# Layer 1's linear attention: mean of the values outside the product, and its products in half-array tiles side by side

## Chip, cores and metric

The kernel runs on one core of a Trainium2 chip. The metric is device time in microseconds, the median over executions. TensorE (PE) multiplies matrices and writes PSUM; VectorE (DVE), ScalarE (ACT) and GpSimd (POOL) do elementwise work; SyncE (SP) only issues transfers here. All data is float32.

## The reference, cut to what matters

Four layers follow each other on `x` of 2 x 512 x 32 x 32: deformable attention with an MLP (layer 0), linear attention (layer 1), and two multi-head attentions behind a group norm (layers 2 and 3). The change is in layer 1:

```python
Q = einsum('oc,bcn->bon', wq, xf) + bq          # 64 x 1024 per batch
K = einsum('oc,bcn->bon', wk, xf) + bk
V = einsum('oc,bcn->bon', wv, xf) + bv          # 512 x 1024
Q = Q / norm(Q, axis=1);  K = K / norm(K, axis=1)
k_sum  = K.sum(-1) + 1e-6
tailor = 1.0 / (n + einsum('bnm,bm->bn', Qt, k_sum))
v_sum  = V.sum(-1)
matrix = einsum('bmn,bcn->bmc', K, V)
matrix_sum = v_sum[:, :, None] + einsum('bnm,bmc->bcn', Qt, matrix)
return x + gamma * (matrix_sum * tailor[:, None, :])
```

The values V are never formed: `matrix` is K times x, and that times the weights of V.

## The kernel before

`xs[b][t]` holds x: two batches, four tiles `t` of 128 channels by 1024 points. A point block `n` is 128 points (eight a batch). The weights of layer 1 lie in `w` as 128 rows x 4 tiles x 640 columns: 512 for V, 64 for Q, 64 for K. The functions are nested in `layer1`, and an order written out by hand at its end fixes what TensorE, ACT and DVE do one after the other (`manual_schedule`); POOL's order and SP's transfers are left to the scheduler.

- `queries_keys(b, half)` (L1062): queries and keys with points on partitions, 16 products for four point blocks; DVE adds the bias, ACT squares.
- `unit_length(b)` (L1084): sums of squares on DVE, square root on ACT, reciprocal on DVE; normed keys `kn` and queries `qn`. Both have a 65th column of ones, so that one product carries the sum of the values along.
- `turned_x(b)` (L1096): x transposed by TensorE, 32 tiles of 128 x 128 a batch; ACT and DVE copy them out, alternately.
- `keys_sum(b)` (L1109) spreads the sum of the keys over all partitions by a product with ones; `keys_column(b)` (L1117) gets the same sum as a column.
- `keys_x(b)` (L1126): x times keys, 32 products with 128 columns of x as weights and the 65 columns of `kn` streamed; result in four tiles `m1`.
- `divisors(b)` (L1143): the divisor of each query, on DVE, and the queries divided by it.
- `turned(b, h)` (L1162) transposes the queries; `matrix(b)` (L1170) multiplies `m1` by the weights of V, 65 rows of 512.
- `result(b, h, t)` (L1181): one product with 65 rows per half and tile. For batch 0 DVE adds it to x, for batch 1 ACT copies it out and POOL adds.

PSUM has three banks in pool `ps`, three in `ps_q`, and two single ones in `ps_m` (tags `m1` and `s`). Interleaved with batch 1 stand the steps of layer 2's group norm on batch 0: `channel_means` (statistics of a tile on DVE), `group_means` (two small products) and `norm_first`, which makes the first operand of layer 2's first product `qk20P`. On POOL the weight sums of layer 2 (L869 to L872) stand before and between the fills of layer 1's constants.

Of the kernel before, what the change touches and what calls it, by code (L numbers as in the profile page):

```python
# [36 lines left out]
    ("gamma1", 1),  # L37
# [19 lines left out]
class Net:  # L57
# [980 lines left out]
    def layer1(self, w, bias):  # L1038
# [3 lines left out]
        with ExitStack() as ctx:  # L1042
# [10 lines left out]
            xT, qk, qn, kn = [], [], [], []  # L1053
            for b in range(B):
                qn.append(pool.tile([P, NB, P], F32, tag=f"qn{b}", name=f"qn{b}"))
                kn.append(pool.tile([P, NB, DH + 1], F32, tag=f"kn{b}", name=f"kn{b}"))
                nc.gpsimd.memset(qn[b][:, :, DH:P], 1.0)
                nc.gpsimd.memset(kn[b][:, :, DH : DH + 1], 1.0)

            sqs = []  # L1060

            def queries_keys(b, half):  # L1062

                if half == 0:
                    qk.append(pool.tile([P, NB, 2, DH], F32, tag=f"qk{b}", name=f"qk{b}"))
                qk_ps = ps_q.tile([P, 4, P], F32, tag="ps", name=f"l1qk{b}{half}")
                for i in range(4):
                    n = 4 * half + i
                    for t in range(CT):
                        xt = self.xs[b][t][:, n * P : (n + 1) * P]  # L1070
                        nc.tensor.matmul(
                            qk_ps[:, i, :], lhsT=xt, rhs=w[:, t, C:640], start=(t == 0), stop=(t == CT - 1)
                        )
                nc.vector.tensor_tensor(
                    qk[b][:, 4 * half : 4 * half + 4, :, :].rearrange("p n a d -> p n (a d)"),
                    qk_ps,
                    bias[:, C:640].unsqueeze(1).to_broadcast([P, 4, P]),
                    ALU.add,
                )
                if half:  # L1080
                    sqs.append(pool.tile([P, NB, 2, DH], F32, tag=f"sq{b}", name=f"sq{b}"))
                    nc.scalar.activation(sqs[b], qk[b], AF.Square)

            def unit_length(b):  # L1084
                r = small.tile([P, NB, 2], F32, tag="r", name=f"r{b}")
                nc.vector.tensor_reduce(r, sqs[b], AX.X, ALU.add)
                nc.scalar.activation(r, r, AF.Sqrt)
                nc.vector.reciprocal(r, r)
                nc.vector.tensor_tensor(
                    kn[b][:, :, 0:DH], qk[b][:, :, 1, :], r[:, :, 1:2].to_broadcast([P, NB, DH]), ALU.mult  # L1090
                )
                nc.vector.tensor_tensor(
                    qn[b][:, :, 0:DH], qk[b][:, :, 0, :], r[:, :, 0:1].to_broadcast([P, NB, DH]), ALU.mult
                )

            def turned_x(b):  # L1096
                xT.append(pool.tile([P, NB, C], F32, tag=f"xT{b}", name=f"xT{b}"))
                for n in range(NB):
# [5 lines left out]
                    (nc.scalar.copy, nc.vector.tensor_copy)[n % 2](xT[b][:, n, :], tr)  # L1104

            vec, act = nc.vector, nc.scalar
            m1, mats, q_at, kbs, kss = [], [], [], [], []

            def keys_sum(b):  # L1109

                kb_ps = ps_m.tile([P, DH + 1], F32, tag="s", name=f"kb{b}")
                for n in range(NB):
                    nc.tensor.matmul(kb_ps, lhsT=ones, rhs=kn[b][:, n, :], start=(n == 0), stop=(n == NB - 1))
                kbs.append(small.tile([P, DH + 1], F32, tag="kb", name=f"kbs{b}"))
                vec.tensor_scalar(kbs[b], kb_ps, 1e-6, None, ALU.add)

            def keys_column(b):  # L1117
                s_ps = ps_m.tile([P, DH + 1], F32, tag="s", name=f"s{b}")
                for n in range(NB):
                    nc.tensor.matmul(  # L1120
                        s_ps[0 : DH + 1, 0:1], lhsT=kn[b][:, n, :], rhs=ones[:, 0:1], start=(n == 0), stop=(n == NB - 1)
                    )
                kss.append(small.tile([DH + 1, 1], F32, tag="ks", name=f"ks{b}"))
                vec.tensor_copy(kss[b], s_ps[0 : DH + 1, 0:1])

            def keys_x(b):  # L1126

                m1_ps = ps_m.tile([P, CT, DH + 1], F32, tag="m1", name=f"m1{b}")
                m1.append(pool.tile([P, CT, DH + 1], F32, tag=f"m1{b}", name=f"m1s{b}"))
                for t in range(CT):  # L1130
                    for n in range(NB):
                        nc.tensor.matmul(
                            m1_ps[:, t, :],
                            lhsT=xT[b][:, n, t * P : (t + 1) * P],
                            rhs=kn[b][:, n, :],
# [3 lines left out]
                    if t == CT - 1:  # L1139
                        act.copy(m1[b], m1_ps)  # L1140
                    yield

            def divisors(b):  # L1143

                prod = pool.tile([P, NB, DH], F32, tag=f"prod{b}", name=f"prod{b}")
                vec.tensor_tensor(
                    prod, qn[b][:, :, 0:DH], kbs[b][:, 0:DH].unsqueeze(1).to_broadcast([P, NB, DH]), ALU.mult
                )
                d = small.tile([P, NB], F32, tag="d", name=f"d{b}")
                vec.tensor_reduce(d, prod, AX.X, ALU.add)  # L1150
                yield
                vec.tensor_scalar(d, d, float(N), None, ALU.add)
                vec.reciprocal(d, d)
                vec.tensor_scalar(d, d, self.col("gamma1"), None, ALU.mult)
                vec.tensor_tensor(
                    qn[b][:, :, 0 : DH + 1],
                    qn[b][:, :, 0 : DH + 1],
                    d.unsqueeze(2).to_broadcast([P, NB, DH + 1]),
                    ALU.mult,
                )  # L1160

            def turned(b, h):  # L1162
                tr = ps_q.tile([P, HF], F32, tag="ps", name=f"qt{b}{h}")
                for n in range(4):
                    nc.tensor.transpose(tr[:, n * P : (n + 1) * P], qn[b][:, 4 * h + n, :], self.ident)
                qa = pool.tile([DH + 1, HF], F32, tag=f"qa{b}{h}", name=f"qa{b}{h}")
                act.copy(qa, tr[0 : DH + 1, :])
                q_at.append(qa)

            def matrix(b):  # L1170
                m_ps = ps_m.tile([DH + 1, C], F32, tag="m1", name=f"m{b}")
                for t in range(CT):
                    nc.tensor.matmul(m_ps, lhsT=m1[b][:, t, :], rhs=w[:, t, 0:C], start=(t == 0), stop=(t == CT - 1))
                mat = pool.tile([DH + 1, C], F32, tag=f"mat{b}", name=f"mat{b}")
                for cut in (slice(0, C // 2), slice(C // 2, C)):
                    vec.scalar_tensor_tensor(
                        mat[:, cut], bias[0 : DH + 1, cut], kss[b], m_ps[:, cut], ALU.mult, ALU.add
# [3 lines left out]
            def result(b, h, t):  # L1181
                w_ps = ps.tile([P, HF], F32, tag="ps", name=f"w{b}{h}{t}")
                nc.tensor.matmul(
                    w_ps, lhsT=mats[b][:, t * P : (t + 1) * P], rhs=q_at[2 * b + h], start=True, stop=True
                )
                xt = self.xs[b][t][:, h * HF : (h + 1) * HF]
                if b == 0:
                    vec.tensor_tensor(xt, w_ps, xt, ALU.add)
                else:

                    ws = last.tile([P, HF], F32, tag="ws", name=f"ws{h}{t}")
                    act.copy(ws, w_ps)
                    nc.gpsimd.tensor_tensor(xt, xt, ws, ALU.add)
# [4 lines left out]
            with self.tc.manual_schedule(engines=engines):  # L1198
                for b, half in ((0, 0), (0, 1), (1, 0)):
                    queries_keys(b, half)  # L1200
                unit_length(0)
                queries_keys(1, 1)
                for b in range(B):
                    turned_x(b)
                unit_length(1)
                keys_sum(0)
                for _ in divisors(0):
                    pass
                for _ in keys_x(0):
                    pass  # L1210
                keys_column(0)
                turned(0, 0)
                matrix(0)
                turned(0, 1)
                keys_sum(1)

                divided, summed = divisors(1), keys_x(1)
                for t in range(CT):
                    for h in range(2):
                        result(0, h, t)  # L1220
                    self.channel_means(2, 0, t)
                    next(summed)
                    if t in (0, 2):
                        next(divided, None)
                next(summed, None)
                keys_column(1)
                turned(1, 0)
                matrix(1)
                turned(1, 1)
                steps = self.group_means(2, 0, ps_m.tile([P, 2, 5 * CT], F32, tag="s", name="gm2"))  # L1230
                next(steps)
                for h in range(2):
                    for t in range(CT):
                        result(1, h, t)
                        if h == 0 and t == 2:
                            next(steps, None)
                        elif h == 1 and t == 1:
                            self.norm_first(2)
# [720 lines left out]
def _layout(i):  # L1959
# [10 lines left out]
    def over(v):  # L1970
# [14 lines left out]
        "gamma1": over(l1["gamma"]),  # L1985
# [45 lines left out]
```

## Time and profile before

| what | value |
|---|---|
| median of 3 runs | 3259.72 us (3259.31 to 3261.21) |
| the profiled execution: time, span | 3260.07 us, 3258.3 us |
| granted TensorE clock in it | 1.0 |
| layer 1 on TensorE | 2342.58 to 2406.57 us |
| busy in 2342.50 to 2406.60: PE, DVE, ACT, POOL | 63.99, 34.48, 16.05, 15.91 us |

The profile is of one execution. Time around the span (start and end of the program) makes the 1.8 us between span and time. A line such as `L1183` is a line of the kernel; `w<-qa,mat` reads as output and inputs; `65*128` is the part of the array that the weights take, `65x512` what is streamed. A float32 product shows as two records, a transpose as one. Matmul records overlap: a record's own duration is longer than the distance to the next, and the distance is what TensorE's time is made of. In the chain of waits a piece has its start, its length and its line.

### The profile page before, as it was taken

To read this page: it belongs to the slowest core of one execution; us is meant where nothing else is said; L and a number is where in the kernel's file an instruction comes from. 1 tells how busy PE (TensorE), PEld (TensorE's weight loads), DVE (VectorE), ACT (ScalarE), POOL (GpSimd) and SP (SyncE) were. 2 spreads that over 40 slices of the span, in tenths; PEclk is the share of its full clock that TensorE was granted. 3 is DMA by queue.
4 is the path that set the end of the run, shared out by engine and by line. 5 is a ranking of instruction groups with operands and counts; after the bars stand their busy time and mean duration, and the time that the engine had idled before them with its cause. 6 is when DMAs were issued, how large, how long until landed. Compare 5 with 4: busy or idle time off the path is not lost.

```text
span 3258.3 us, 59109 instructions
## 1 busy us (share of the span) xinstructions
PE 3243.6 (100%) x24496; PEld 1210.7 (37%) x24496; DVE 2388.4 (73%) x2742; ACT 1949.1 (60%) x2013; POOL 2348.2 (72%) x1557
## 2 busy tenths in 40 slices
PE   9999999999999999999999999999999999999999
PEld 4333333333333333332333334444555533455333
DVE  7877878878877778878877765475555689855897
ACT  7787887887886687887887752111121466213662
POOL 7998998999998698999999972442323458634575
PEclk9999999999999999999999999999999999999999
DMA  6676776667766476667676662111000100000001
GB/s 171 144 152 136 152 148 143 146 146 146 149 145 127 104 153 139 142 143 146 149 145 145 145 158 78 39 39 39 1 1 1 40 1 2 14 1 14 1 1 53
DMA packets 96571, 309.35 MB, mean 95 GB/s; under 512 B 14688, under 2 KB 16864, under 8 KB 93216
## 3 DMA queue, kind: packets, MB, share of 16 engines
q0 software_dynamic: 57040, 200.31, 32.5%
q1 hardware_dynamic: 38240, 103.05, 9.7%
q8 instruction: 197, 3.23, 0.4%
q10 hardware_dynamic: 1008, 2.06, 0.2%
q14 instruction: 86, 0.70, 0.1%
HBM read 67.33 MB, written 4.46 MB: 22 GB/s over the span
## 4 chain that ended last, share of the span: by engine, by line
PE 81%; POOL 11%; DVE 5%; issue 2%; ACT 0%; DMA 0%; DVEq 0%; POOLq 0%; ACTq 0%; SPq 0%
PE hp L704 41%; PE s L1569 5%; PE o L1598 5%; POOL h L723 5%; POOL h L720 4%; PE qk30P L1344 1%; PE qk20P L1344 1%; PE m_7P L899 1%; PE m_6P L899 1%; PE m_4P L899 1%; PE m_2P L899 1%; PE m_0P L899 1%; PE qk31P L1344 1%; PE qk21P L1344 1%; PE m_5P L899 1%
## 5 line engine op out<-in xcount | busy, mean ns | idle before, releaser
L704 PE MATMUL hp<-h,w2s 128*32 128x512 f32 x16384 | 1784.0, 592 | 0.5 <-DVE h L680 0.2
L680 DVE CUSTOM_DVE_ANT_1 h<-tx,bank 128x1024 f32<-128x1024 f32 (+1 forms) x1028 | 1180.3, 1210 | 301.9 <-PE hp L704 240.3
L709 ACT ACTIVATE h<-hp,magb 128x1024 f32<-128x1024 f32 x1024 | 1133.1, 1110 | 378.8 <-PE hp L704 368.2
L704 PEld LDWEIGHTS hp<-h,w2s 128*32 128x32 f32 x16384 | 530.6, 110 | 1212.5 <-issue 1184.6
L720 POOL TENSOR_TENSOR h<-h,h 128x1024 f32<-128x1024 f32 x255 | 819.1, 3212 | 1.6 <-ACT h L709 1.6
L723 POOL TENSOR_TENSOR h<-h,h 128x1024 f32<-128x1024 f32 x254 | 751.3, 2958 | 0.0
L716 POOL DMA_DIRECT2D h<-h x255 | 303.0, 1188 | 192.3 <-ACT h L709 179.6
L1573 ACT ACTIVATE e<-s 128x1024 f32<-128x1024 f32 x256 | 262.0, 1025 | 181.1 <-PE s L1569 176.5
L711 ACT ACTIVATE h<-h,flip 128x1024 f32<-128x1024 f32 x256 | 294.3, 1150 | 8.4
L1598 PE MATMUL o<-e,v 64*64 64x512 f32 x2048 | 265.2, 589 | 2.2 <-DVE q L1637 2.2
L1569 PE MATMUL s<-q,k 64*64 64x512 f32 x2048 | 265.9, 591 | 0.0
L1580 POOL TENSOR_TENSOR some<-some,e 128x1024 f32<-128x1024 f32 x64 | 168.2, 2629 | 26.2 <-ACT e L1573 23.3
L1578 POOL TENSOR_TENSOR some<-e,e 128x1024 f32<-128x1024 f32 x32 | 76.1, 2379 | 141.3 <-DVE sum L1587 102.3
L726 POOL DMA_DIRECT2D h<-h x127 | 175.4, 1381 | 1.0 <-issue 1.0
L725 POOL DMA_DIRECT2D h<-h x127 | 149.0, 1173 | 0.0
L1585 DVE TENSOR_TENSOR sum<-sum,e 128x1024 f32<-128x1024 f32 x64 | 124.6, 1947 | 28.8 <-ACT e L1573 26.1
L869 POOL TENSOR_TENSOR mlp_w<-mlp_w 128x512 f32<-128x512 f32 x16 | 22.3, 1391 | 165.0 <-DMA mlp_w<-in_mlp_w 111.2
L1598 PEld LDWEIGHTS o<-e,v 64*64 64x64 f32 x2048 | 77.8, 133 | 145.1 <-issue 134.9
L1569 PEld LDWEIGHTS s<-q,k 64*64 64x64 f32 x2048 | 76.5, 133 | 133.2 <-issue 117.5
L960 ACT ACTIVATE mh<-mh,cols 128x512 f32<-128x512 f32 x64 | 46.1, 721 | 124.3 <-DVE mh L978 65.4
L1583 DVE TENSOR_TENSOR sum<-e,e 128x1024 f32<-128x1024 f32 x32 | 81.5, 2547 | 31.7 <-ACT e L1573 31.6
L1332 POOL TENSOR_TENSOR sq<-q 128x512 f32<-128x512 f32 x32 | 33.2, 1041 | 96.1 <-DVE q L1351 54.2
(572 smaller groups left out, 3365.2 us busy)
## 6 DMA issues: line engine op xcount, KB each, us to landing
h<-h POOLq DMA_DIRECT2D x255, 512.0 KB, 5.4
h<-h POOLq DMA_DIRECT2D x254, 256.0 KB, 5.0
h<-h SPq DMA_DIRECT2D x127, 256.0 KB, 4.0
lb<-logs SPq DMA_DIRECT2D x63, 512.0 KB, 5.6
mlp_w<-in_mlp_w SPq DMA_DIRECT2D x16, 1024.0 KB, 4.9
x<-in_x SPq DMA_DIRECT2D x8, 512.0 KB, 7.5
qkw<-in_l_qk SPq DMA_DIRECT2D x2, 2048.0 KB, 7.7
out<-x SPq DMA_DIRECT2D x15, 256.0 KB, 2.0
```

Of the source, the lines that this page charges most:

```text
L680: self.nc.vector._custom_dve(TENSOR_ADD_SAT, out=h1[r][:, k, cut, :], in0=x[:, 4 * half + 2 * r + k, :].unsqueeze(1).to_broadcast([P, H // ...
L704: nc.tensor.matmul(hp[rows, cut], lhsT=self.l0w2[:, 32 * q : 32 * q + 32], rhs=h1[k][:, cut], start=True, stop=True)
L709: nc.scalar.activation(y, hp, AF.Relu, bias=self.magb[:, q, 0:1])
L711: nc.scalar.activation(y, y, AF.Copy, scale=self.flip)
L716: nc.gpsimd.dma_start(y, ys[0], accum_op=ALU.add)
L720: (nc.vector if final else nc.gpsimd).tensor_tensor(y, y, ys[2], ALU.add)
L723: (nc.vector if final else nc.gpsimd).tensor_tensor(z, z, other, ALU.add)
L726: nc.gpsimd.dma_start(z[1::2, :], z[0::2, :], accum_op=ALU.add)
L899: self.nc.tensor.matmul(acc[p], lhsT=w[:, a, k, p * P : (p + 1) * P], rhs=right(r, k), start=k == 0, stop=k == 1)
L1569: nc.tensor.matmul(s[halves[c], par, :], lhsT=ks[p][rows, at : at + DH], rhs=qs[p][rows, cut], start=True, stop=True)
L1573: nc.scalar.activation(e, s, AF.Exp, scale=DH**-0.5)
L1598: nc.tensor.matmul(o[halves[par], r, :], lhsT=v[n // 2][rows, n % 2, at : at + DH], rhs=e[rows, par, :], start=(n == 0), stop=(n == NB - 1),)
```

## The change

The sum of the values no longer rides along as row 65. With c the mean of x over the points, V's sum is n times (wv c + bv), and the result is gamma (wv c + bv) plus gamma times the divided queries times a matrix that is built from x - c. ACT takes minus the means (`means_less`), `means_row` and `means_columns` turn them into the constant column `rest` that is added with the result, and `centred` subtracts the means' share from keys times x. Keys and queries then have 64 columns, and `keys_x`, `matrix` and `result` are each two products on halves of the array. In `keys_x` and `matrix` the halves are two groups of 64 columns; in `result` they are two groups of 64 rows, for which the divided queries are written twice. Divisors move to POOL (`divided`), batch 0's tiles 2 and 3 are added on ACT and POOL, batch 1's tiles 0 and 1 on DVE. The order by hand is new.

```diff
-            qn.append(pool.tile([P, NB, P], ...)); kn.append(pool.tile([P, NB, DH + 1], ...))
-            nc.gpsimd.memset(qn[b][:, :, DH:P], 1.0)
-            nc.gpsimd.memset(kn[b][:, :, DH : DH + 1], 1.0)
+            less = pool.tile([P, CT, 32], F32, tag="less", name="l1less")
+            gps.memset(less, 0.0)
...
+            def means_less(b):
+                for t in range(CT):
+                    act.activation(spare, self.xs[b][t], AF.Copy, scale=-1.0 / N, accum_out=less[:, t, b : b + 1])
...
-            def keys_column(b):
...
+            def divided(b):
+                prod = sqs[b][:, :, 0, :]
+                gps.tensor_tensor(prod, qk[b][:, :, 0, :], kbs[b].unsqueeze(1).to_broadcast([P, NB, DH]), ALU.mult)
+                d = small.tile([P, NB], F32, tag="d", name=f"d{b}")
+                vec.tensor_reduce(d, prod, AX.X, ALU.add)
+                vec.tensor_scalar(d, d, float(N), None, ALU.add)
+                vec.reciprocal(d, d)
+                vec.tensor_scalar(d, d, self.col("gamma1"), None, ALU.mult)
+                qn.append(pool.tile([P, NB, 2, DH], F32, tag=f"qn{b}", name=f"qn{b}"))
+                for i in range(2):
+                    gps.tensor_tensor(
+                        qn[b][:, :, i, :], qk[b][:, :, 0, :], d.unsqueeze(2).to_broadcast([P, NB, DH]), ALU.mult
+                    )
...
             def keys_x(b):
-                for t in range(CT):
-                    for n in range(NB):
+                for n in range(NB):
+                    for half in range(2):
                         nc.tensor.matmul(
-                            m1_ps[:, t, :],
-                            lhsT=xT[b][:, n, t * P : (t + 1) * P],
-                            rhs=kn[b][:, n, :],
+                            m1_ps[half * DH : (half + 1) * DH, :],
+                            lhsT=kn[b][:, n, :],
+                            rhs=xT[b][:, n, half * 2 * P : (half + 1) * 2 * P],
...
+            def centred(b):
+                tr = ps_m.tile([P, 2, P], F32, tag="m1", name=f"m1t{b}")
+                for j in range(2):
+                    nc.tensor.transpose(tr[:, j, :], m1[b][:, j * P : (j + 1) * P], self.ident)
+                m1[b] = pool.tile([P, CT, DH], F32, tag=f"m1c{b}", name=f"m1c{b}")
+                for t in range(CT):
+                    vec.scalar_tensor_tensor(
+                        m1[b][:, t, :], kbs[b], less[:, t, b : b + 1],
+                        tr[:, t % 2, (t // 2) * DH : (t // 2 + 1) * DH], ALU.mult, ALU.add,
+                    )
...
             def matrix(b):
-                    nc.tensor.matmul(m_ps, lhsT=m1[b][:, t, :], rhs=w[:, t, 0:C], start=(t == 0), stop=(t == CT - 1))
+                    for half in range(2):
+                        nc.tensor.matmul(
+                            m_ps[half * DH : (half + 1) * DH, :],
+                            lhsT=m1[b][:, t, :],
+                            rhs=w[:, t, half * 2 * P : (half + 1) * 2 * P],
...
+            def means_row():
+                got = ps_m.tile([P, C], F32, tag="s", name="l1row")
+                for t in range(CT):
+                    nc.tensor.matmul(
+                        got[32 * t : 32 * t + 32, :], lhsT=less[:, t, :], rhs=w[:, t, 0:C], start=True, stop=True
+                    )
...
+            def means_columns(row):
+                got = ps_m.tile([P, CT, B], F32, tag="s", name="l1cols")
+                for t in range(CT):
+                    nc.tensor.matmul(got[:, t, :], lhsT=row[:, t * P : (t + 1) * P], rhs=pick, start=True, stop=True)
+                for b in range(B):
+                    vec.tensor_tensor(rest[:, b, :], self.colr("vb1", CT), got[:, :, b], ALU.subtract)
+                vec.tensor_scalar(rest, rest, self.col("gamma1"), None, ALU.mult)
+
+            def result(b, j, h):
+                for half, to in enumerate((ps, ps_q)):
+                    t = 2 * half + j
+                    rows = slice(half * DH, (half + 1) * DH)
+                    w_ps = to.tile([P, HF], F32, tag="ps", name=f"w{b}{h}{t}")
+                    nc.tensor.matmul(
+                        w_ps, lhsT=mats[b][rows, j * P : (j + 1) * P], rhs=q_at[2 * b + h][rows, :], start=True, stop=True
+                    )
+                    xt = self.xs[b][t][:, h * HF : (h + 1) * HF]
+                    more = rest[:, b, t : t + 1]
+                    if half == 0:
+                        vec.scalar_tensor_tensor(xt, w_ps, more, xt, ALU.add, ALU.add)
+                    else:
+                        ws = last.tile([P, HF], F32, tag="ws", name=f"ws{b}{h}{t}")
+                        act.activation(ws, w_ps, AF.Identity, bias=more)
+                        gps.tensor_tensor(xt, xt, ws, ALU.add)
...
+                queries_keys(0, 0)
+                means_less(0)
+                queries_keys(0, 1)
+                queries_keys(1, 0)
                 unit_length(0)
+                means_less(1)
                 queries_keys(1, 1)
+                keys_sum(0)
+                turned_x(0, range(NB))
                 unit_length(1)
+                divided(0)
+                keys_x(0)
+                row = means_row()
+                turned_x(1, range(0, 4))
+                centred(0)
+                keys_sum(1)
+                turned_x(1, range(4, NB))
+                matrix(0)
                 turned(0, 0)
                 turned(0, 1)
+                means_columns(row)
+                divided(1)
+                for j in range(2):
+                    for h in range(2):
+                        result(0, j, h)
+                keys_x(1)
+                for t in (0, 2):
+                    self.channel_means(2, 0, t)
                 turned(1, 0)
+                turned(1, 1)
+                centred(1)
+                for t in (1, 3):
+                    self.channel_means(2, 0, t)
                 matrix(1)
                 steps = self.group_means(2, 0, ps_m.tile([P, 2, 5 * CT], F32, tag="s", name="gm2"))
+                result(1, 0, 0)
                 next(steps)
+                result(1, 0, 1)
+                next(steps, None)
+                result(1, 1, 0)
+                self.norm_first(2)
+                result(1, 1, 1)
```

The packed table `cols` of per-channel constants gains the four columns of V's bias (`vb1`), 156 in place of 152.

## The prediction

> **What bounds the kernel now.** I read the page first. TensorE is busy for the whole span, and the chain that ended last runs 81% on it.
>
> ```profile
> PE 3243.6 (100%) x24496; PEld 1210.7 (37%) x24496; DVE 2388.4 (73%) x2742; ACT 1949.1 (60%) x2013; POOL 2348.2 (72%) x1557
> PE 81%; POOL 11%; DVE 5%; issue 2%; ACT 0%; DMA 0%; DVEq 0%; POOLq 0%; ACTq 0%; SPq 0%
> ```
>
> The change lies in layer 1, so next the chain cut to the stretch between the last MLP product and the first two products of layer 2.
>
> ```profile
> 2342.58 14.29 PE l1qk L1071 x128
> 2356.87 6.99 PE l1t L1101 x64
> 2363.86 1.73 PE kb L1113 x16
> 2365.59 7.15 PE m L1132 x64
> 2372.74 0.89 PE s L1120 x16
> ...
> 2374.13 3.43 PE m L1173 x8
> ...
> 2399.24 2.81 PE w L1183 x6
> 2402.05 0.12 PE gm L1493 x2
> 2402.18 4.40 PE w L1183 x10
> 2406.57 6.44 PE qk20P L1344 x15
> ```
>
> Layer 1 is 2342.58 to 2406.57, 64.0 us, with one piece (0.11 us) that is not a product: TensorE alone sets its length. A float32 product is two records here, a transpose one. Pitches: 128 columns of weights cost 0.11 us however little streams past (7.15 / 64), 512 streamed columns 0.43 us (3.43 / 8). So the stage gets shorter by what TensorE loses, until a product has to wait. What could make it wait is read from the other engines' timelines:
>
> ```profile
> 2347.16 2.36 POOL L871 TENSOR_TENSOR qkm<-qkw 128x1024 f32<-128x1024 f32 x1
> 2349.46 0.20 POOL L1052 MEMSET l1ones<- 128x128 f32 x1
> 2350.49 1.06 ACT L1082 ACTIVATE sq<-qk 128x1024 f32<-128x1024 f32 x1 [27.83 <-DVE qk L1074]
> 2351.56 1.28 ACT L1087 ACT_TABLE_LOAD   x1
> ```
>
> POOL reaches layer 1's fills only at 2349.5, behind layer 2's weight sums; ACT is idle for 27.83 us before the first square. Last, how fast products go that use half or a quarter of the array:
>
> ```profile
> L704 PE MATMUL hp<-h,w2s 128*32 128x512 f32 x16384 | 1784.0, 592 | 0.5 <-DVE h L680 0.2
> 67.31 1.15 PE L580 MATMUL bank<-w,xnT 128*64 128x64 f32 x32
> 2590.69 1.04 PE L1598 MATMUL o<-e,v 64*64 64x512 f32 x8
> 2591.66 0.43 PE L1626 MATMUL d<-part,same 128*128 128x64 f32 x2
> 2592.02 1.09 PE L1569 MATMUL s<-q,k 64*64 64x512 f32 x8
> ```
>
> L704 (32 columns each) takes 1784.0 / 16384 = 0.109 us a record, a quarter of 0.43: four run at once. L580 is the case of this change, two 64-column products over all rows with 64 columns streamed: 32 records in 1.15 us, 0.04 each, where a single 64-column stream takes 0.05 (half of the 0.11 for 128) and so 1.7. The quadrants of L1598 and L1569 (8 in 2 x 0.43) show row halves running together too.
>
> **TensorE's sum, part by part** (us, both batches).
> - `queries_keys` 14.3, `turned_x` 7.0, `keys_sum` 3.5, `turned` 1.9: same counts, same pitch.
> - `keys_x`: 128 records of 0.11 (14.3) become 64 of 256 streamed columns. L1363 streams 256 in 0.22; two side by side make 32 slots x 0.216 = 6.9.
> - `keys_column` (2 x 0.89) goes.
> - `matrix`: 16 x 0.43 = 6.9 becomes 16 slots x 0.216 = 3.5.
> - `result`: 32 records, 14.1 with their reloads, become 16 slots x 0.429 = 6.9.
> - New: `means_row`, eight records in four column groups, 2 slots, 0.9; `means_columns` 8 x 0.11 = 0.9; transposes in `centred` 4 x 0.11 = 0.4. Group means stay 0.2.
>
> Before 64.0, after 46.3.
>
> **Changing tile shape[...].** Layer 1 had whole-array products only; now the shape changes 15 times. The three lines around L1626 price it: the last slot of L1598 ends at 2590.69 + 2 x 0.43 = 2591.55, the next shape-64 product starts at 2592.02, and 0.22 of that 0.47 is the two records themselves. That leaves 0.25 for two changes, 0.13 each, 2.0 us in all. [...] I take the row: 46.3 + 2.0 = 48.3.
>
> **The new waits.** The work that hid everything is now 16 us shorter, so each hand-over has to be followed. I walked through the changed kernel's instruction order, engine by engine, adding up these rows' durations (hand-over to TensorE 0.13 us, from TensorE 0.035 after the record's end). The same walk through the kernel before reaches layer 2 0.5 us early.
> 1. `means_less(0)` stands ahead of the square on ACT. Its target `less` is filled by POOL after L871 and `ones`, at 2349.9, so it can't use ACT's idle time; the square and everything that ACT does later is queued behind it. A 128x1024 activation with a running sum is not in the trace. Nearest: L1082, 1.06, and the scaled copy L711, 1.15. Low end 1.09 (1.06 and a hand-over, sum free); high end 1.35 (a small ACT record like the early square root, 0.20, to read the sum out). I take 1.23 with hand-over, between. Four end at 2354.8; square 1.06, DVE reduce 1.21 (the table load hides here), root 0.22, reciprocal 0.25, keys 0.69: 2358.4. `keys_sum(0)` is due on TensorE at 2356.87: **waits 1.65**.
> 2. Behind the root ACT runs `means_less(1)`, 4 x 1.23, and the second square, before its copies of x's transposes. Their buffers are three; the seventh tile finds none free: **waits 1.1**, until 2364.0.
> 3. From there TensorE runs through to `centred(1)` at 2387.14. POOL's divisors (each 128x512 step at 1.27, L1193's row) end at 2372.5 and 2383.2, needed at 2377.0 and 2386.1: hidden, with 2.9 us to spare for the second. At 1.6 a step (their operands are broadcast, which no row of POOL's shows) 0.5 us more would be lost, through the additions to tile 2 and the statistics that wait for them ahead of step 4; a step shorter than 1.27 gains nothing. DVE's division of their sums and the eight `rest` columns lie beside `means_columns` and `result(0)`. ACT's `row` copy and the x additions on POOL are likewise covered until step 4.
> 4. `matrix(1)` follows its own transposes at once, so DVE's four small steps (0.17 to 0.25) are bare: **waits 1.0**.
> 5. DVE then takes the statistics of tiles 1 and 3 (2 x 1.49) before it scales the matrix; that is done at 2391.8, and `result(1,0,0)`, due at 2389.9, **waits 1.8**. Those statistics lay under the products of batch 1 before.
> 6. The norm of layer 2's first block comes behind four result additions on DVE and ends at 2397.5; TensorE is through at 2396.4: **waits 1.25**. POOL's last addition ends at 2399.4, and the second block's norm at 2400.2, well ahead of its product at 2404.5.
>
> Waits 6.8; 48.3 + 6.8 = 55.1 against 64.0, a gain of 8.9. The walk's miss of 0.5 before, partly shared by both, makes it 8.7. SP's queue issues what it did; `cols` grows by four columns in 152, under 0.1 us. From layer 2 on nothing but TensorE leads the chain, so the gain stays.
>
> **Rivals.**
> - *The tiles take turns.* If the halves don't overlap in these shapes (64 rows by 128 columns is in no row of the trace), keys, matrix, result and row cost 37.9 in place of 18.1; the waits shrink, and the walk reaches layer 2 at 2415.0, 8.5 late: 3268.2. It turns the sign where about half of the overlap is missing. L580 and L704 speak against it. 5%.
> - *Packing pays less.* [...] L704's 0.109 is within 2% of a quarter, so I don't take it. A dearer sum (1.35), change (0.20) and POOL (1.3 times) together give 6.3: 3253.4. With both, 15%.
> - *The early waits are not there.* With `less` filled in time, step 1's wait vanishes and 2 stays: layer 2 at 2395.9; cheaper sums or changes bring about as much. Gain 10.5 to 11.5: 3248.2 to 3249.2. 15%.
>
> **How the numbers follow.** Main case, 65%: the profiled execution took 3260.07 (span 3258.3 and 1.8 around it); less 8.7 is 3251.4. The median of the runs shown is 0.35 lower, so 3251.0. The range goes from 3247.8, the early-wait case with cheap changes, to 3255.3, the packing case. 0.2%, 6.5 us, is about what a measurement of this kernel can tell from no change. Main and early cases pass it, with a small part of the second rival: faster 0.81; the rest of that rival 0.14; the turns 0.05.
>
> **What would show it.** In the profile after: `keys_x` in pairs, 3.5 us a batch; idle time of TensorE before `kb` on DVE's keys, before the seventh transpose on ACT, before the second `m` and first `w1` on DVE's matrix steps, and before `qk20P` on the norm; shape changes of 0.13. Layer 2's first product at 2397.7. It is wrong if TensorE idles over 10 us there, if paired records start 0.2 us apart or more, or if layer 2 grows.

## The result, and the profile after

| | before | changed |
|---|---|---|
| median of 9 runs each | 3259.72 us (3259.31 to 3261.38) | 3251.05 us (3250.27 to 3252.71) |
| profiled execution: time, span | 3260.07, 3258.3 us | 3251.48, 3249.7 us |
| layer 1 on TensorE, up to `qk20P` | 2342.58 to 2406.57: 63.99 us | 2342.28 to 2397.98: 55.70 us |
| from there to the end of the span | 851.7 us | 851.7 us |

The ratio is 0.9973 (95% interval 0.9963 to 0.9984). All of the difference of the two spans is in layer 1 (8.3 us) and in its start, which this execution reached 0.3 us earlier; layers 2 and 3 take what they took. The page of the changed kernel, the lines that answer to the first ones shown of before:

```profile
PE 3230.7 (99%) x24436; PEld 1200.2 (37%) x24436; DVE 2388.3 (73%) x2745; ACT 1960.0 (60%) x2032; POOL 2351.6 (72%) x1563
PE 80%; POOL 11%; DVE 6%; issue 2%; ACT 1%; DMA 0%; DVEq 0%; POOLq 0%; ACTq 0%; SPq 0%
```

TensorE is no longer busy for the whole span, and DVE and ACT have each won a point of the chain. Where, the chain of waits shows for the stretch that was TensorE's alone (start, length, what):

```profile
2349.50 0.15 POOL l1less L1056
2349.67 1.16 ACT l1spare L1089 x2
...
2354.37 0.95 ACT sq L1084
2355.33 1.28 ACT L1094
...
2357.16 0.70 DVE kn L1097
2357.86 0.14 issue
2358.00 1.97 PE kb L1117 x16
2359.97 5.17 PE l1t L1108 x32
2365.13 3.60 PE m L1141 x32
2368.74 1.00 PE l1row L1200 x8
...
2375.34 1.88 PE m L1181 x16
...
2379.02 3.66 PE w L1221 x16
...
2388.43 1.21 DVE stats L1517 x2
...
2391.26 0.28 DVE mat L1191
...
2397.08 0.76 DVE xn L1568
```

`keys_x` is the `m` of L1141: 3.60 us where the kernel before took 7.15. `matrix` is 1.88 where it took 3.43, and the results of batch 0 (`w`, L1221) take 3.66, where the kernel before took 2.81 + 4.40 = 7.2 for those of batch 1. At the front the chain leaves TensorE for POOL's fill, four passes of means on ACT, the square and the keys, as step 1 of the prediction has it; at the end for DVE's statistics (step 5) and the norm (step 6). TensorE's own timeline gives the waits in brackets:

```profile
2358.00 1.97 PE L1117 MATMUL kb<-kn,l1ones 128*128 128x64 f32 x16 [1.26 <-DVE kn L1097]
2359.80 5.33 PE L1108 MATMUL l1t<-ident,x 128*128 128x128 f32 x32
...
2388.57 1.95 PE L1181 MATMUL m<-l1w,m1c 128*64 128x256 f32 x16 [1.04 <-DVE m1c L1158]
2391.68 1.48 PE L1221 MATMUL w<-qa,mat 64*128 64x512 f32 x4 [1.16 <-DVE mat L1191]
...
2397.98 2.38 PE L1385 MATMUL qk20P<-xn,qkw 128*128 128x512 f32 x5 [1.20 <-DVE xn L1568]
```

Four waits stand where the prediction put them. One line fits nothing: 32 transposes in 5.33 us without any bracket, where 32 at 0.11 are 3.5. The prediction had a wait for ACT's copies there (step 2). A table by stretches (time, busy us of PE, PEld, DVE, ACT and POOL with counts, granted clock, share and rate of the DMA) shows another cause:

```profile
2356.50:2359.90 3.40, 2.14 (x20) 1.98 (x19) 2.21 (x5) 3.33 (x7) 0.00 (x0) 1.00 0.00 0
2360.00:2363.30 3.30, 3.30 (x17) 3.30 (x16) 0.92 (x2) 3.27 (x7) 1.27 (x1) 0.50 0.00 0
2363.40:2366.80 3.40, 3.40 (x32) 2.69 (x32) 2.95 (x4) 1.17 (x2) 0.00 (x0) 1.00 0.02 5
```

The granted clock (the third number from the end) is 0.50 in the middle row: TensorE gets through 17 transposes where the same time holds 30 at full clock. The clock's entries in the trace put the drop at 2359.94, for 3.413 us. No drop lies in layer 1 of the profile before.

### The profile page after: what moved, and what is told of

Its sections match the earlier page's. It is cut to its first block, busy times and chain, and to the rows that moved or that the text cites. A ratio compares the mean times of both kernels' runs of the same rounds, so it can differ in the third digit from the quotient of the medians.

```text
span 3249.7 us, 59022 instructions
## 1 busy us (share of the span) xinstructions
PE 3230.7 (99%) x24436; PEld 1200.2 (37%) x24436; DVE 2388.3 (73%) x2745; ACT 1960.0 (60%) x2032; POOL 2351.6 (72%) x1563
## 4 chain that ended last, share of the span: by engine, by line
PE 80%; POOL 11%; DVE 6%; issue 2%; ACT 1%; DMA 0%; DVEq 0%; POOLq 0%; ACTq 0%; SPq 0%
PE hp L704 41%; PE s L1610 5%; PE o L1639 5%; POOL h L723 4%; POOL h L720 4%; PE qk30P L1385 1%; PE qk20P L1385 1%; PE qk21P L1385 1%; PE m_6P L899 1%; PE m_4P L899 1%; PE m_2P L899 1%; PE m_0P L899 1%; PE qk31P L1385 1%; PE m_5P L899 1%; PE m_3P L899 1%
## 5 line engine op out<-in xcount | busy, mean ns | idle before, releaser
L1373 POOL TENSOR_TENSOR sq<-q 128x512 f32<-128x512 f32 x32 | 33.2, 1039 | 99.2 <-DVE q L1392 55.1
```

## The experiments

Two kinds of loss had to be told apart: waits for another engine, and the clock. The lengths below run from layer 1's first product to `qk20P`, in one profile each.

| kernel | layer 1, us | clock at 0.50 within it | median |
|---|---|---|---|
| before | 63.99 | none | 3259.72 |
| changed, first profile | 55.70 | 3.41 us from 2359.94 | 3251.05 |
| changed, second profile | 54.56 | none | |
| changed, third profile | 56.64 | 6.83 us from 2393.13, to just past its end | |
| early fill | 55.10 | 6.83 us from 2391.04, to just past its end | 3248.57 |
| early fill, both means first | 54.27 | 3.41 us from 2390.82 | 3248.91 |
| halves in turn | 62.24 | 3.41 us from 2359.29 | 3256.95 |
| shapes mixed | 59.03 | 3.41 us from 2396.09 | 3253.88 |
| waits filled with products | 54.58 | none | 3250.05 |
| other order at the end | 53.54 | none | 3249.40 |
| both means first + order | 51.64 | none | 3247.60 |
| the same, waits filled | 51.64 | none | 3247.78 |

### The changed kernel twice more

No edit. 

> The changed kernel as it is, for a second profile. Theory A (idle time of TensorE drops its clock[...]): with 1.3 us idle ahead of keys_sum(0) and three more waits of 1.0 to 1.2 near the end, a drop is likely but at another place than 2359.9, or absent; where it does not meet the transposes of batch 0, these take 3.9 to 4.1 us with a wait of about 0.45 for ACT's copy; layer 2 starts 54.5 us behind layer 1 without a drop, 55.2 to 56.2 with one. Theory B (the transposes themselves run at half pitch behind the square and the means): 5.3 us for them again, with no drop or the same one.

> The same once more, a third profile of the changed kernel: by theory A the place of the drop, and with it the length of layer 1 (54.5 without, 55.2 to 56.2 us with one), is another again or there is none; by theory B it is the stretch of the transposes in each.

Measured: in the second profile there is no drop at all, and the transposes behind `keys_sum(0)` show the wait of step 2, in TensorE's timeline:

```profile
2360.72 2.79 PE L1108 MATMUL l1t<-ident,x 128*128 128x128 f32 x24
2363.81 1.09 PE L1108 MATMUL l1t<-ident,x 128*128 128x128 f32 x8 [0.30 <-ACT xT L1111]
```

Six tiles run through, the seventh waits for ACT. From start to start that is 0.47 us over the normal pitch. In the third profile the transposes look the same, and the clock is 0.50 near the end of the layer:

```profile
2393.20:2399.90 6.70, 6.35 (x15) 2.26 (x16) 3.79 (x14) 3.11 (x6) 3.79 (x3) 0.50 0.00 0
```

So one program gives three lengths, 54.56, 55.70 and 56.64 us; the last lies above the 55.2 to 56.2 expected with a drop, because its drop is twice as long. The place changes as theory A has it, and B (the transposes themselves are slow) falls. That idle time is what drops the clock is not shown by these two profiles. The 54.56 is the length to compare orders with.

### Early fill

```diff
-            gps.memset(less, 0.0)
...
+                vec.memset(less, 0.0)
                 queries_keys(0, 0)
                 means_less(0)
```

> One edit to the changed kernel: the target of the means is filled by DVE at the head of layer 1's order, not by POOL behind layer 2's weight sums. means_less(0) can then run in ACT's idle time and the first square is free at about 2350.4. In the changed kernel's trace TensorE lost 1.26 us before keys_sum(0) and then 1.7 us within the transposes of x behind it, whose pitch was 0.213 in place of 0.109 us. Theory A: that second loss is the TensorE clock, granted at 0.50 for 3.41 us after the idle time, and goes with it; what comes instead is the seventh transposed tile's wait for ACT (means_less(1) still stands there), about 0.6. Layer 2 then starts 2.3 us earlier (2395.7 instead of 2398.0), median about 3248.7, and the 32 transposes take about 4.1 us. Theory B (step 2 of the prediction): the second loss is the wait for ACT's copies and stays; 1.3 us earlier, median about 3249.8, the 32 transposes still take 5.2 us or so. Theory C: another wait of the same length stands behind the first, nothing gained: 3251.

Measured: 3248.57 us (3248.36 to 3250.64). TensorE's timeline:

```profile
2356.76 1.90 PE L1116 MATMUL kb<-kn,l1ones 128*128 128x64 f32 x16
2358.49 2.79 PE L1107 MATMUL l1t<-ident,x 128*128 128x128 f32 x24
2361.57 1.09 PE L1107 MATMUL l1t<-ident,x 128*128 128x128 f32 x8 [0.29 <-ACT xT L1110]
```

The wait ahead of `keys_sum(0)` is gone, and the seventh tile's stays at 0.45 from start to start. Up to the first result of batch 1 the layer takes 46.75 us; the second profile of the changed kernel takes 48.26. The gain is 1.5, near the 1.4 of the wait alone. So the fill's place in POOL's queue was the cause of that wait. What theory A said of the clock came half true: the drop left the transposes, but this profile has a longer one at the end, where the other three waits still stand, and layer 2 starts at 2397.6, not 2395.7. The expectation had mistaken one profile's place of the drop for the kernel's, and its median, 3248.7, came out for a reason that was wrong in part.

### Both batches' means ahead of the first square

```diff
-            gps.memset(less, 0.0)
...
+                vec.memset(less, 0.0)
                 queries_keys(0, 0)
                 means_less(0)
+                means_less(1)
...
                 unit_length(0)
-                means_less(1)
```

> As with the early fill, and means_less(1) too stands before the first square, so that all eight passes of means lie in ACT's idle time and its copies of the transposes have nothing ahead of them. The first square is then about 2.4 us late (2352.8), which costs nothing, since DVE is held by the bias of the third quarter until 2353.9 anyway. Theory A (clock): the whole 2.9 us go, clock 1.00 throughout, the 32 transposes in 3.5 us, layer 2 at 2395.1, median about 3248.1; against the early fill alone only some 0.6 us better. Theory B (ACT's copies were the second loss): also 2.9 us in all, but then the early fill alone shows at most half of it. Theory C: means on ACT before the square delay the keys again by up to 1 us: 3249 to 3250.

Measured: 3248.91 us (3248.21 to 3249.97), the early fill's time within the spread. In the trace the transposes behind `keys_sum(0)` are back at 3.6 us without a wait:

```profile
2358.44 3.66 PE L1107 MATMUL l1t<-ident,x 128*128 128x128 f32 x32
```

Up to the first result of batch 1 the layer takes 46.38, 0.37 less than with the early fill; by the trace, not by the medians, that is a gain. The keys come no more than 0.07 us later than with the early fill, so the late square costs next to nothing, and C falls. A's full clock did not come: a drop of 3.41 us lies near the end of this profile too.

### Halves in turn

```diff
-                for n in range(NB):
-                    for half in range(2):
+                for half in range(2):
+                    for n in range(NB):
```

The same for `t` in `matrix`. 

> One edit to the changed kernel: in keys_x and matrix all steps of the lower half run first, then all of the upper half, so that neighbouring products never lie in different halves of the array. The same products, columns and results, only their order. Theory A (the overlap of the halves is the gain): 32 records of 0.216 us in place of 16 slots, keys_x 6.9 us in place of 3.6 and matrix 3.5 in place of 1.9, 10 us in both batches; about 1 us comes back because matrix(1) now covers DVE's statistics: layer 2 about 9 us later, median about 3260, that of the kernel before. Theory B (the gain is the exchange of operands, 64 records where there were 128, and the dropped column): the order matters little, median below 3253.

Measured: 3256.95 us (3255.93 to 3258.18). B falls, and A is 3 us too high:

```profile
2364.56 6.32 PE L1141 MATMUL m<-xT,kn 128*64 128x256 f32 x32
...
2377.40 2.86 PE L1181 MATMUL m<-l1w,m1c 128*64 128x256 f32 x16
```

32 records of 0.216 would be 6.9 us, not 6.3. The record starts show why: twelve lie about 0.216 apart, then four pairs, then twelve more 0.216 apart. Those around the seam, in us:

```
2366.985  2367.200  2367.206  2367.417  2367.473  2367.633  2367.689  2367.848  2367.905  2368.120  2368.336
```

At the seam the first four records of the upper half ran beside the last four of the lower one, though they stand behind them in the order (the records don't name their half; that is read from their number and spacing). `matrix` has four pairs as well. The overlap in the changed kernel is therefore worth (6.25 - 3.60) + (2.79 - 1.88) = 3.6 us a batch from start to start, 7.1 in both, and 10.6 if none of the four had crossed the seam (16 x 0.216 more). DVE's `mat` was waited for 0.60 in place of 1.16, so 0.56 came back of the 1 us expected. Without any overlap in these two steps the layer would be about as long as before (54.56 + 10.6 - 0.56 = 64.6, an estimate), though the results' row halves stayed in pairs in this run. So the gain rests on the overlap, and the exchange of operands alone brings nothing. That the row halves overlap is seen in their pitch alone: 16 records in 3.66, 0.23 each, where 512 streamed columns took 0.43 in the kernel before.

### Shapes mixed

```diff
-                keys_x(0)
+                keys_x(0, turned_pairs(1, range(0, 4)))
                 row = means_row()
-                turned_x(1, range(0, 4))
```

> One edit to the changed kernel: the sixteen transposes of x that stood behind keys_x(0) stand inside it, two after each of its eight steps, which changes the tile shape 15 times more. Theory A (0.13 to 0.14 us a change: 0.09 more at the last product of a shape and 0.05 at the first of the next, as the changed kernel's trace shows them): 2.0 to 2.1 us later, and up to 0.3 because the copy of the sums stands behind one more copy on ACT: layer 2 at 2400.1 to 2400.4, median about 3253.3. [...] Theory C (a change is free, and the gaps at the seams have other causes): 3251.

Measured: 3253.88 us (3252.72 to 3256.10). TensorE's timeline, one turn of eight and the start of the next:

```profile
2364.57 0.65 PE L1156 MATMUL m<-xT,kn 128*64 128x256 f32 x4
2365.15 0.44 PE L1107 MATMUL l1t<-ident,x 128*128 128x128 f32 x2
2365.52 0.65 PE L1156 MATMUL m<-xT,kn 128*64 128x256 f32 x4
...
2373.95 2.00 PE L1130 MATMUL kb<-kn,l1ones 128*128 128x64 f32 x16 [0.32 <-ACT l1rows L1221]
```

A turn takes 0.95 us, and its products 2 x 0.216 + 2 x 0.109 = 0.65: 0.30 for two changes, 0.15 each. Over the whole stretch the mixed order takes 7.61 us where the products and the transposes one after the other take 3.60 + 1.80: 2.2 us for 15 changes. That is a little above the prediction's 0.13 and the 0.13 to 0.14 of A; C falls. Up to `keys_sum(1)` this order takes 2.76 us more than the changed kernel's second profile. The other 0.5 is a wait at another place, and longer, than the 0.3 that the expectation allowed: `keys_sum(1)` shares its PSUM buffer with `means_row`, whose copy now stands late on ACT (the last line above). With that wait in it, the median lies 0.6 above A's 3253.3 and can't give the price of a change; the turn of eight does.

### Waits filled with products

```diff
+            def warm(tag, n):
+                got = ps_m.tile([P, P], F32, tag=tag, name="warm")
+                for _ in range(n):
+                    nc.tensor.matmul(got, lhsT=ones, rhs=ones, start=True, stop=True)
...
+                warm("s", 5)
                 keys_sum(0)
...
+                warm("s", 4)
                 matrix(1)
+                warm("s", 4)
...
                 result(1, 1, 1)
+                warm("m1", 4)
```

> The changed kernel with useless products in TensorE's four waits: 128x128 ones times ones, five ahead of keys_sum(0), four each ahead of matrix(1), behind matrix(1) and behind the last result (about 0.9 to 1.1 us each, a little less than the waits). Nothing waits less, no work is removed. Theory A (short idle times make the clock drop to 0.50 for 3.41 us somewhere in the next microseconds): the granted clock stays 1.00 from 2342 to layer 2 in the profile, the transposes behind keys_sum(0) take 4.0 us (a wait of 0.45 for ACT's copy stays, as with the early fill) in place of 5.3, layer 2 starts 55.7 - 1.2 = 54.5 us after layer 1; over the timed runs the highest come down, the median 0 to 1 us below 3251.05. Theory B (the drop has nothing to do with the idle time, but with the kind of work): a drop of 3.41 us is there as before, median 3251. Theory C (the fillers themselves delay the work behind them): up to 0.5 us later.

Measured: 3250.05 us (3249.54 to 3251.14); TensorE's timeline:

```profile
2357.62 1.28 PE L1067 MATMUL warm<-l1ones 128*128 128x128 f32 x10
2359.06 1.97 PE L1122 MATMUL kb<-kn,l1ones 128*128 128x64 f32 x16 [0.17 <-DVE kn L1102]
2360.87 2.79 PE L1113 MATMUL l1t<-ident,x 128*128 128x128 f32 x24
2363.96 1.10 PE L1113 MATMUL l1t<-ident,x 128*128 128x128 f32 x8 [0.30 <-ACT xT L1116]
```

54.58 us, the length of the changed kernel without a drop, to 0.02. The fillers cost nothing and removed no wait, so C falls. Whether A or B holds is not settled. One profile without a drop proves little, as the second profile of the changed kernel has none either. The median is 1.0 below the changed kernel's, but it is also 0.8 below the median of those of its runs that kept the full mean clock (3250.89), so drops explain little of that 1.0.

The runs say a little more. Each comes with its mean clock, rounded. In the first profile of the changed kernel it is 0.99912: the drop of 3.41 us takes 0.00053, and another 2.3 us at 0.50 at the end of the span, from 3247.41, take 0.00035. In the profile before, with 0.4 us at the end alone, it is 0.99994. So one drop makes 0.999 of 1.000, and the end of the execution can blur it. With the long waits left in (changed, early fill, both means, halves in turn, mixed) 22 of 56 runs show 0.999; with the waits filled, or shortened as in the combination below, 0 of 16. In the three kernels that have most of them, the runs at 0.999 are 0.9 to 1.2 us longer in the median. Two things weaken this. The 16 ran on another chip than four of those five kernels; on their chip the order with only its end changed (below), whose wait of 1.28 at the front stands, shows 0.999 in 1 of 6 runs. And the kernel before, which has no such waits in layer 1, shows it in 7 of 47 (these 1.3 us longer in the median), in a place that no profile caught; 0 of 16 is not clear of that.

Waits of the same length also stand where no profile has a drop. TensorE's waits in the whole of the kernel before (for which product, released by what, us in total, times, longest):

```profile
PE qk30P L1344 <- issue: 1.6, 1, 1.6
PE sim L742 <- DMA h<-h: 1.2, 1, 1.2
```

Both stand in every profile of this document, 1.15 or 1.16 us in layer 0 (`sim`) and 1.55 ahead of layer 3 (`qk30P`), and the clock stays at 1.00 behind them in all twelve.

### Another order at the end, and all together

```diff
-                for t in (0, 2):
+                for t in (0, 1):
                     self.channel_means(2, 0, t)
                 turned(1, 0)
-                turned(1, 1)
                 centred(1)
-                for t in (1, 3):
-                    self.channel_means(2, 0, t)
+                self.channel_means(2, 0, 2)
+                turned(1, 1)
                 matrix(1)
+                self.channel_means(2, 0, 3)
...
                 result(1, 0, 0)
+                add = result(1, 0, 1, True)
                 next(steps)
-                result(1, 0, 1)
+                add()
+                add = [result(1, 1, 0, True)]
                 next(steps, None)
-                result(1, 1, 0)
+                add.append(result(1, 1, 1, True))
                 self.norm_first(2)
-                result(1, 1, 1)
+                for a in add:
+                    a()
```

With `True`, `result` only issues its products; the additions follow where the returned function is called. 


> The changed kernel with another order at the end of layer 1, the same work: statistics of tiles 0 and 1 first, the transposes of batch 1's sums between the two transposes of its queries, tile 2's statistics under matrix(1), tile 3's behind its scaling, and of the results' additions on DVE only the first two ahead of layer 2's norm. Theory A (waits 4 to 6 of the prediction are an order on DVE, not its work): the wait ahead of matrix(1) falls from 1.04 to 0.5, that ahead of the first result from 1.16 to 0.5, that ahead of qk20P to under 0.6: layer 2 starts about 1.8 us earlier, median about 3249.3. Theory B (DVE is the bound there, what one wait loses the next gains): at most 0.6 us, 3250.5 or more.

Measured: 3249.40 us (3248.22 to 3250.30). The layer takes 53.54, 1.0 less than 54.56: between A and B. The waits became 0.60, 0.60 and 1.06 where they were 1.04, 1.16 and 1.20. About half of the two on DVE's matrix steps was the order's. The last is not DVE's load but a row of small steps behind the second group-mean product (ACT's `sc`, then five steps of 0.1 to 0.2 and the norm on DVE, 2.1 us from the end of `gm` to `qk20P` in the combination below).

> The early fill with both batches' means ahead of the first square, and the new order at the end. If the two add up: 2.3 us for the first and 1.8 for the second, median about 3247.1; if the gain at the front is used up by waits at the end: 3248 to 3249.

Measured: 3247.60 us (3247.26 to 3247.85), against before 0.9962 (0.9948 to 0.9975), and 3.45 us less than the changed kernel. Layer 1 takes 51.64: 54.56 less 1.9 for the means (48.26 - 46.38 up to the first result of batch 1) and 1.0 for the end. The two gains add up. TensorE's timeline has no bracket before these:

```profile
2385.44 1.95 PE L1180 MATMUL m<-l1w,m1c 128*64 128x256 f32 x16 [0.60 <-DVE m1c L1157]
2387.99 2.34 PE L1221 MATMUL w<-qa,mat 64*128 64x512 f32 x8 [0.60 <-DVE mat L1190]
...
2394.14 4.10 PE L1395 MATMUL qk20P<-xn,qkw 128*128 128x512 f32 x9 [1.06 <-DVE xn L1578]
```

The same with products in these three waits:

> As the combination, with useless products in the three waits that are left at the end (two of 128x128 ahead of matrix(1) and behind it, four behind the last result). Theory A (idle time drops the clock): clock 1.00 through layer 1 and into layer 2, median 0 to 0.7 us below the combination, about 3246.7, and a smaller spread. Theory B: no difference. Theory C: the fillers delay, up to 0.4 us above the combination.

Measured: 3247.78 us (3247.18 to 3247.95), layer 1 51.64: theory B of that run, no difference. The combination's profile has no drop, and none of its 5 runs shows the lower mean clock, so there was nothing to prevent.

## Why the prediction was right, and where it was not

The time (3251.05 for 3251.0) and the mechanism were right: the halves overlap, and 15 us less on TensorE (63.99 to 49.1) uncover waits that take back about a third. That the sum came out so close is luck: its errors cancel (waits 1.3 too long, products 0.8 too short), and the median holds what was not in it. Runs with a drop of the clock are among the nine (four show 0.999, with a median of 3252.08 against 3250.89 for the others), and the start of layer 1 alone differs by up to 1.6 us between the profiles (2341.75 to 2343.32). Waits are counted from start to start over the normal pitch, in the profile without a drop for all but the clock.

| step | predicted, us | measured, us |
|---|---|---|
| TensorE's products and changes of shape | 48.3 | 49.1 |
| 1. `keys_sum(0)` for the means on ACT | 1.65 | 1.43 |
| 2. seventh transpose for ACT's copy | 1.1 | 0.47 |
| 4. `matrix(1)` for DVE's steps | 1.0 | 1.1 |
| 5. `result(1,0,0)` behind two tiles' statistics | 1.8 | 1.2 |
| 6. `qk20P` for the norm | 1.25 | 1.3 |
| layer 1 without a drop of the clock | 55.1 | 54.56 |
| drops of the clock | not seen | 0 to 2.1, by the execution |

- **Paired records.** `keys_x` 3.60 and `matrix` 1.88 a batch for predicted 3.46 and 1.73 and a change; `means_row` 1.0 for 0.9; batch 0's results, row halves in pairs, 3.66 for 3.43. The rivals in which tiles take turns or pack worse have nothing in the trace: `keys_x` takes 3.60 / 16 = 0.225 us a pair, with its changes of shape, where one record alone takes 0.216. The packing case, which sets the upper end of the prediction's range (3255.3), was the author's assumption, and no trace of before shows it. The 0.05 for a single stream of 64 columns was an estimate, half of the 0.11 for 128. That 128 columns of weights cost 0.11 however little streams past was taken from 65 streamed columns; in `means_columns`, with 2, records start 0.11 us apart as well, but for the first step (0.03).
- **Changes of shape.** 0.15 each by the mixed order, not 0.13: 2.2 us, 0.2 more. Of the other 0.6 by which TensorE's sum was low, 0.36 is the first result of batch 1. DVE scales `mat` in two steps, one a half, and TensorE starts the lower half's product behind the first of them: in the second profile at 2391.45, and the upper half's at 2391.82, so that these two are no pair. Their four records take 1.42 us up to `gm`, the next four 1.06. Another 0.07 is a first product behind a wait (`keys_sum(0)` 1.81 from start to start, `keys_sum(1)` 1.73); the parts of the prediction's sum add up to 46.4, not 46.3. The small rest isn't assigned.
- **Step 1.** A pass of means is 1.06 and a separate read-out of the sum, 0.19, at a pitch of 1.18, inside the bounds of 1.09 to 1.35 and under the 1.23 taken. The table load hid less well than said: it ends at 2356.61, with DVE's reduce (2356.57), so that the two are level. The hand-over of the keys to TensorE took 0.14 (2357.86 to 2358.00) for the 0.13 taken.
- **Step 2** and step 5 are the terms that were mis-sized most. Step 2 is 0.47 for 1.1, and in the first profile it is not seen: there the half clock makes the transposes slower than ACT's copies.
- **Step 3.** POOL's two multiplications by the broadcast divisor take 1.02 each (2.04 together), not 1.27 and not the 1.6 that the prediction assumed for its dear case; its product with the sum of the keys takes 1.27. Batch 1's ended at 2382.97 for transposes at 2386.22. Hidden, as said.
- **Step 5** was 0.6 too long. The two tiles' statistics took 2.83 on the chain (2388.43 to 2391.26) for 2.98, and `matrix(1)` with its changes of shape 1.88 for 1.73, so that the product was due later: 0.3 of it. The other 0.3 is about one of the two steps in which DVE scales `mat` (0.36): the prediction speaks of the scaling as one step, and the first product waits for one half of it only.
- **The early-wait rival** (gain 10.5 to 11.5, 3248.2 to 3249.2) is what the early fill then gave, 3248.57; it was not what this kernel does.
- **The clock.** That "TensorE alone sets its length" had held with TensorE busy throughout; that its clock might not stay at 1.0 was not asked. The gain of 8.9 in the layer is 9.4 without a drop; in the changed kernel's profiles a drop takes 1.1 (3.41 us over the transposes, where it replaces the 0.47) or 2.1 (6.83 us).

## What to carry to other kernels

When a change takes work off the engine that had hidden everything, walk every hand-over that it covered, and look first for an instruction that waits for something trivial (here a fill behind another layer's work on POOL) with a long queue behind it; mending that and the order at the end gave another 3.45 us. Order half-array tiles in the loop so that neighbouring products lie in different halves: here the other order lost two thirds of the overlap (7.1 of an estimated 10.6 us). Compare orders by a stretch of the trace with the same clock in it, and by more than one profile, since an effect of 1 to 2 us can be the clock's (1.1 and 2.1 here).

## What the hardware did that had not been expected

- **TensorE's clock halves for a while in layer 1, and why there stays open.** A drop takes 3.413 us in the first profile of the changed kernel, 3.41 in three others and 6.83 in two. In that first profile and in the one before, every change of the clock lies a whole number of 3.4133 us (2355.196 / 690) behind the trace's first clock entry, to 0.006 us: 690, 691 and 950 times in the changed kernel, 953 in the one before (950 and 953 lie behind TensorE's last product). In all six profiles with a drop, the 3.41 us ahead of its start hold one whole wait of 1.16 to 1.29 us; the second half of the two long drops has no such wait ahead of it. The reverse does not hold. TensorE's timelines show 17 waits of that length in layer 1, in eight profiles, and six of them stand so ahead of a drop. In the third profile the wait of 1.28 ahead of `keys_sum(0)`, up to 2358.78, lies whole in a stretch of 3.413 us counted back from the drop (2355.58 to 2359.00), and no drop follows. The second profile and the one with another order at the end have four of the 17 and no drop in layer 1, and none follows the waits for `sim` (1.15 or 1.16) and `qk30P` (1.55) in any profile. So a wait of this length is not enough by itself. What work stands around it may count as well, and no run here tells.
- **Records of the other half seem to start ahead of their turn.** In the halves-in-turn kernel four records of the upper half, it seems, ran beside the last four of the lower one, in `keys_x` and in `matrix`. In `keys_x` the first of the four pairs starts at 2367.200 and 2367.206, the last at 2367.848 and 2367.905. If the early ones are the upper half's, as their number and spacing suggest, the first of them started 0.64 us before a record that stands ahead of it in the order.
- **A change of tile shape** costs 0.15 us in this kernel: about 0.09 at the last record of the old shape and 0.05 at the first of the new one. In the first profile, at the start of `keys_x`, the last transpose takes 0.202 us up to the next start (0.109 otherwise), and the first pair 0.268 (0.216 otherwise).
